# Half of batch one's MLP moved from between the attention units to the seven-product stage behind attention, in a cross-attention block on one Trainium2 core

## The chip, the core and the metric

The kernel runs on one core of one Trainium2 chip. The metric is device time in microseconds (us) of one execution. Five engines work from instruction queues of their own, each in program order: TensorE (PE, matmuls), VectorE (DVE), ScalarE (ACT), GpSimd (POOL) and SyncE (SP, which here only issues DMAs). ACT and POOL issue a few DMAs too. An instruction waits for its inputs and for its output buffer, and everything behind it on its engine waits with it.

## The reference

For each of 4 batches, with 512 queries, 512 keys, width 512, 16 heads of 32 and an inner width of 2048, all in float32:

```python
x = layer_norm(hidden_states, ln1_w, ln1_b)
q, k, v = x @ q_w + q_b, enc @ k_w + k_b, enc @ v_w + v_b      # split into 16 heads
attn = softmax(where(mask, q @ k.T / sqrt(32), min))
hidden = (attn @ v) @ cproj_w + cproj_b + hidden_states
y = layer_norm(hidden, ln2_w, ln2_b)
return hidden + gelu(y @ fc_w + fc_b) @ proj_w + proj_b
```

## The kernel before

**Units, quarters, pairs.** Attention is cut into 16 units w: batch w // 4, and four of the 16 heads. A unit has four quarters of 128 queries; u = 4w + quarter counts them from 0 to 63. In a quarter (`scores`, L233) PE makes the scores of the four heads (`sc`, L240, one PSUM tile of four banks, single-buffered); DVE adds the mask and finds the row extreme (L245); ACT takes the exponential (L249); DVE turns the result in 32x32 blocks into the tile `tb` (`turn`, L253, L277). Two quarters make a **pair** p = 2w + half, with 256 queries.

**The exchange.** The blocks of `tb` lie on the wrong partitions, so the turned pair is copied within on-chip memory by 16 DMAs of 136 KB (`copies`, L305 to L320, all issued by SP), into a tile that `attend` (L342) then multiplies with v (`av`, L362). Pairs 2, 4, 6 are copied into `gt`, pairs 29 and 31 into `xe`; **every other one goes into the tile `pT`, of which there is one**. So `exchange` (L294) holds the next pair's copies back until `attend` of the pair before is through: its last step, the DVE multiply `oT` (L367), reads the last rows of `pT`, and SP's first copy waits for it. `attend` of pair p stands ahead of the scores of quarter 2p + 4 (LAG, L60, L853); for pairs 7 and up that is one `attend` per half unit.

**Work between the units.** Everything else on PE is cut into pieces of four 128x512 matmuls into one PSUM tile, here called **chains**: k, q and v of coming units (L196, L206, L218), the output projection `accc` (L399), and the MLP of batches 0 and 1, `accf` (`fc`, L457) and `accp` (`proj`, L467), 64 chains. The profile counts each f32 matmul as two, so a chain has 8. The lists `first[w]` and `later[w]` (L773 to L843) say which chains a unit gets (`some(n)` takes the next n of the MLP), and the loop at L845 hands them out over the quarters by cost: `CHAIN` is 3.4, a turn of layer norm 0.5. Of the 64 MLP chains 57 stand in units 5 to 15, 7 behind the last unit. MLP weights come in tiles of 256 KB, eight at a time; a chain that has read the last of one lets SP load the next (`load_mlp`, L442).

**Behind attention** (`last_mlps`, L515) batches 2 and 3 are done by seven products of blocks in place of eight: `fc_pair` (L549) makes two of the 16 inner blocks by 14 matmuls of 128x256 (`q`, L561), `project` (L592) the projection by seven products (q1p to q7p, L601). The sums of blocks that this needs are made by DVE: `sum_wa` (fc weights), `y_sums`, `g_sums`, `p_sums` (projection weights). `project` ends with the work for the next batch: after q5p, `middle` queues `y_sums` and `sum_wa(0)` on DVE, PE does q4p, and the third product of the next `fc_pair` reads `s4`, the last result of `sum_wa(0)`.

**Before the last stage** PE does, in this order: 2 MLP chains, `attend` of pair 30, 4 chains, `attend` of pair 31, 1 chain, the four `accc` of batch 3.

Of the kernel before, what the change touches and what calls it, by code (L numbers as in the profile page):

```python
# [55 lines left out]
AHEAD = 3  # L58
NORMAL = 2
LAG = 4  # L60
# [14 lines left out]
def xattn_block(ctx: ExitStack, tc: tile.TileContext, x, encT, mask, q_w, k_w, v_w, c_w, fc_w, p_w, vecs, rows, out):  # L75
# [10 lines left out]
    att = ctx.enter_context(ExitStack())  # L86
    one, two, kqp, five, six, fws = pools(att, one=1, two=2, kqp=4, five=5, six=6, fws=MW)
    ps_sc = att.enter_context(tc.tile_pool(name="ps_sc", bufs=1, space=PSUM))
# [14 lines left out]
    gT = [gt[:, i * FQ * L : (i + 1) * FQ * L].rearrange("p (k l) -> p k l", k=FQ) for i in range(2)]  # L103

    S = {}
    Q = [nc.sync]

# [73 lines left out]
    def load_w(w, queue=None, names=("wk", "wq", "wv")):  # L181

        if w >= NW:
            return
        g = w % NG
        for n, src in (("wk", k_w), ("wq", q_w), ("wv", v_w)):
            if n in names:
                S[n, w] = two.tile([P, ND, P], F32, tag=n, name=f"{n}_{w}")
                (queue or Q[0]).dma_start(out=S[n, w], in_=src[:, g, :, :])

    def prep_k(w):
        b, g = divmod(w, NG)
        kT = kqp.tile([P, L], F32, tag="kT", name=f"kT_{w}")
        acc = acc_tile(f"acck_{w}")
        for d in range(ND):
            nc.tensor.matmul(acc, S["wk", w][:, d, :], eT[:, d, :], start=(d == 0), stop=(d == ND - 1))  # L196
        load_w(w + 2, names=("wk",))
        nc.scalar.activation(kT, acc, AF.Identity, bias=vec[:, KB + g : KB + g + 1], scale=1.0)
        S["kT", w] = kT

    def prep_q(w):
        b, g = divmod(w, NG)
        qT = kqp.tile([P, L], F32, tag="qT", name=f"qT_{w}")
        acc = acc_tile(f"accq_{w}")
        for d in range(ND):
            nc.tensor.matmul(acc, S["wq", w][:, d, :], xT[:, d, :], start=(d == 0), stop=(d == ND - 1))  # L206
        load_w(w + 2, names=("wq",))

        nc.scalar.activation(qT, acc, AF.Identity, bias=qb[:, g : g + 1], scale=-scale)  # L209
        S["qT", w] = qT  # L210
# [22 lines left out]
    def scores(w, qt):  # L233
# [8 lines left out]
        for h in range(HG):  # L242
            s = six.tile([P, L], F32, tag="s", name=f"s_{w}_{qt}_{h}")
            mn = small.tile([P, 1], F32, tag="mn", name=f"mn_{w}_{qt}_{h}")
            nc.vector.tensor_tensor_reduce(  # L245
                out=s, in0=sc[:, h, :], in1=S["mb", w // NG], scale=1.0, scalar=FMAX,
                op0=ALU.add, op1=ALU.min, accum_out=mn,
            )
            nc.scalar.activation(s, s, AF.Exp, bias=mn, scale=-1.0, accum_out=sums[:, qt, h : h + 1])  # L249
            ps.append(s)  # L250
# [125 lines left out]
    def stays(b, t):  # L376

        return b == 0 or b < B - 1 and t < 2

    def load_h(b, *ts_):  # L380
# [3 lines left out]
        for t in ts_:  # L384
            pool, tag = (hids, "hid") if stays(b, t) else (tiles, "xn")
            S["h", b, t] = pool.tile([P, D], F32, tag=tag, name=f"h_{b}_{t}")
            Q[0].dma_start(out=S["h", b, t], in_=x[b, ts(t, P), :])
            if stays(b, t):
                S["hid", b, t] = S["h", b, t]
# [5 lines left out]
    def cproj(b, t):  # L395
# [5 lines left out]
        if not stays(b, t):  # L401
            (nc.sync if b == B - 1 else nc.gpsimd).dma_start(out=S["xa", b][ts(t, P), :], in_=h)

    def load_hid(b, ts_):
# [28 lines left out]
    weights, products = [], []  # L433
    for b in range(NORMAL):
        for name, q in (("fc", 0), ("fc", 1), ("p", 0), ("fc", 2), ("p", 1), ("fc", 3), ("p", 2), ("p", 3)):
            for k in range(FQ):
                last = len(products) + (k if name == "fc" else NT - 1)
                weights.append((name, b, q * FQ + k, last))
            products += [(name, b, q, k) for k in range(FQ)]
    count = [0, 0]  # L440

    def load_mlp():  # L442

        while count[0] < len(weights) and (count[0] < MW or weights[count[0] - MW][3] < count[1]):
            name, b, f, _ = weights[count[0]]
            w = fws.tile([P, D], F32, tag="mw", name=f"{name}w_{b}_{f}")
            if name == "fc":
# [63 lines left out]
    def sum_wa(c):  # L511
        a = wa[c % 2]
        a_sums(a[:, 0, :2], a[:, 0, 2:], a[:, 1, :2], a[:, 1, 2:], *(ws[c % 2][:, i] for i in range(4)))

    def last_mlps():  # L515
        last, ring = pools(ctx, last=1, ring=2)
# [3 lines left out]
        gs = last.tile([P, 3, NP, HL], F32, tag="gs", name="gs")  # L520
        pb = last.tile([P, NP, 2, D], F32, tag="pb", name="pb")
        pt = last.tile([P, 3, NP, HL], F32, tag="pt", name="pt")
        hl = last.tile([P, NT, D], F32, tag="hl", name="hl")
        p1p, u2p, u3p = (last.tile([P, 2, HL], F32, tag=n, name=n) for n in ("p1p", "u2p", "u3p"))

# [11 lines left out]

        def p_sums(c):

            c = slice(c, c + 2)  # L540
            b11, b12, b21, b22 = (pb[:, c, k, j * HL : (j + 1) * HL] for k in range(2) for j in range(2))
            b_sums(b11, b12, b21, b22, pt[:, 0, c], pt[:, 1, c], b12, pt[:, 2, c])

        def g_sums(c):
# [3 lines left out]

        def fc_pair(b, c, sums):  # L549
            a11, a12, a21, a22 = (wa[c % 2][:, i, 2 * k : 2 * k + 2] for i in range(2) for k in range(2))  # L550
# [23 lines left out]

            if c == 0:
                product(q43[:, 1], s4, y22)
# [7 lines left out]
            gelu(1, 1, uc[:, 0])  # L584
            if c:
                product(q43[:, 1], s4, y22)
# [4 lines left out]

        def project(b, sums, turns, middle):  # L592
            g11, g12, g21, g22 = (ga[:, :, k, j * HL : (j + 1) * HL] for j in range(2) for k in range(2))
# [4 lines left out]
            def product(o, a, w, ts_=range(2)):  # L598
                for t in ts_:
                    for c in range(NP):  # L600
                        nc.tensor.matmul(o[:, t], a[:, c, ts(t, P)], w[:, c], start=(c == 0), stop=(c == NP - 1))  # L601

# [46 lines left out]

        y_sums(NORMAL)  # L650
        for t in range(NT):
            S["hid", B - 1, t] = hl[:, t]
        for b in range(NORMAL, B):
            for c in range(NP):
                if b == NORMAL:
                    for i in range(2):
                        nc.sync.dma_start(out=pb[:, c, i, :], in_=p_w[ts(2 * c + i, P), :])
                fc_pair(b, c, lambda: sum_wa(c + 1) if c + 1 < NP else None)
                if c + 2 < NP:
                    load_wa(c + 2)  # L660
                elif b + 1 < B:
                    load_wa(c + 2 - NP)
                if c % 2 == 0 and c:
                    g_sums(c - 2)

                if b + 1 < B:
                    for t in {0: (0,), 1: (1, 2), 3: (3,)}.get(c, ()):
# [6 lines left out]

            def sums(b=b):
                if b == NORMAL:
                    for c in range(0, NP, 2):
                        p_sums(c)
                if b + 1 < B:
                    load_hid(b + 1, range(NT))  # L680

            def turns(b=b):
                if b + 1 < B:
                    run(turns2(b + 1))

            def middle(b=b):
# [3 lines left out]

            project(b, sums, turns, middle)

# [89 lines left out]
    mlp = []  # L782
    for p in range(NORMAL):
        mlp += FC(p, 0) + FC(p, 1) + PJ(p, 0) + FC(p, 2) + PJ(p, 1) + FC(p, 3) + PJ(p, 2) + PJ(p, 3)

    def some(n):
# [31 lines left out]
    k, q, v = A(8)  # L818
    first[5] = norm(0, 0, 1, 2, 3) + [q, k] + t2[:3] + [v] + t2[3:] + pb_(0) + some(5)
    k, q, v = A(9)  # L820
    x1, x2, x3, x4 = inputs(3)
    first[6] = [k, q] + some(5) + [v] + x1
    k, q, v = A(10)
    first[7] = [k, q] + x2[:1] + some(3) + x2[1:2] + some(3) + [v]

# [3 lines left out]
    k, q, v = A(12)  # L829
    first[9] = [q] + some(2) + [k] + some(3) + [v]  # L830
    k, q, v = A(13)
    first[10] = [k, q] + some(5) + [v]
    k, q, v = A(14)
    t2 = turns2(1)
    first[11] = stat(1, 0, 1) + [k, q] + stat(1, 2, 3) + rs(1) + some(2) + norm(1, 0, 1) + some(1)
    first[11] += norm(1, 2, 3) + some(2) + t2 + pb_(1) + [v]

    k, q, v = A(15)
    first[12] = h_(2, 2, 3, 0, 1) + [k] + some(3)
    later[12] = cb(2) + C(2)  # L840
    first[13] = hid_(1, 2, 3) + [q] + some(3) + [v] + some(3)
    first[14] = some(5) + stat(2, 0, 1) + some(2) + stat(2, 2, 3) + rs(2) + some(1)
    first[15] = norm(2, 0, 1) + some(4) + norm(2, 2, 3) + some(4) + turns2(2) + pb_(2)  # L843

# [31 lines left out]

    load_h(B - 1, *range(NT))
    run(some(2))
    turn_sums(NW - 1, 0)
    attend(NW - 1, 0)  # L880
    run(some(2))
    load_wa(0)
    run(some(2))
    turn_sums(NW - 1, 1)
    attend(NW - 1, 1)
    run(some(2))
    load_wa(1)
    sum_wa(0)
    c_bias(B - 1)
    run(C(B - 1))  # L890
    load_hid(NORMAL, (2, 3))
    att.close()
# [45 lines left out]
```

## Time and profile before

| | |
|---|---|
| median of 3 runs | 826.09 us (825.77 to 826.44) |
| the profiled execution | 823.17 us, its span 821.4 us |
| PE | 805.0 us busy, 98% of the span |
| DVE, ACT, POOL | 562.7, 347.7, 90.4 us busy |
| DMA | 134.91 MB, mean 164 GB/s |
| units 1 to 15, start of the first scores to the end of the last | 52.26 to 572.0 us |
| stage of seven products | 622.7 to 818.1 us |

The profile is of one execution. Its page gives busy time by engine and by 40 equal slices, and the chain that ended last, followed back from the last instruction. The trace behind it answers for a stretch of time with the instructions of one engine, and ahead of each the idle time and what ended it. A PE matmul's listed length is longer than its spacing, since matmuls are pipelined; lengths here are differences of starts.

### The profile page before, as it was taken

What the parts mean: (1) busy time and instruction counts of PE and PEld (TensorE: products, weight loads), DVE (VectorE), ACT (ScalarE), POOL (GpSimd) and SP (SyncE); (2) the same over time, 40 slices, a digit from 0 to 9 for tenths busy, and PEclk for the clock granted to TensorE, in tenths of its full rate; (3) what the DMA queues carried; (4) which work ended last, traced back from release to release, by engine and by line L of the source; (5) the groups of instructions that cost most, each with busy time, mean ns of one, the idle gap of its engine ahead of it and who ended that gap; (6) DMA issues with size and microseconds to landing.
All of it is one profiled execution on the core that took longest, in us unless ns stands there. A gap on an engine that the chain in (4) does not pass through costs nothing.

```text
span 821.4 us, 11900 instructions
## 1 busy us (share of the span) xinstructions
PE 805.0 (98%) x4020; PEld 467.0 (57%) x4020; DVE 562.7 (69%) x1264; ACT 347.7 (42%) x741; POOL 90.4 (11%) x98
## 2 busy tenths in 40 slices
PE   9998999999999999999999999999999999999998
PEld 6553545454454554454544444434447888888887
DVE  3598989886576778667886667787426986268511
ACT  2455555346554744365435367556201331023200
POOL 1110003112000111000111210010201012200011
PEclk9998999999999999999999999999999999999999
DMA  9639998856668768677676676777734550023001
GB/s 327 231 88 237 239 247 233 218 147 161 173 164 222 183 166 237 162 209 194 159 212 179 157 197 159 199 181 174 211 116 162 193 171 14 26 77 89 2 13 39
DMA packets 59740, 134.91 MB, mean 164 GB/s; under 512 B 12144, under 2 KB 14320, under 8 KB 59552
## 3 DMA queue, kind: packets, MB, share of 16 engines
q1 hardware_dynamic: 58416, 130.73, 58.8%
q0 software_dynamic: 736, 2.29, 0.8%
q10 hardware_dynamic: 528, 1.14, 0.5%
q8 instruction: 32, 0.52, 0.3%
q14 instruction: 28, 0.23, 0.1%
HBM read 58.74 MB, written 6.29 MB: 79 GB/s over the span
## 4 chain that ended last, share of the span: by engine, by line
PE 85%; DMA 5%; DVE 5%; SPq 3%; issue 1%; ACT 1%; DVEq 0%; ACTq 0%
PE accp L467 14%; PE accf L457 14%; PE q L561 12%; PE sc L240 7%; PE accc L399 7%; PE av L362 6%; PE accv L218 4%; PE acck L196 4%; PE accq L206 4%; SPq L319 3%; PE q4p L601 2%; PE q3p L601 2%; PE q7p L601 2%; PE q2p L601 2%; PE q5p L601 2%; PE q6p L601 2%
## 5 line engine op out<-in xcount | busy, mean ns | idle before, releaser
L249 ACT ACTIVATE s<-s,mn 128x512 f32<-128x512 f32 x256 | 181.6, 710 | 138.0 <-DVE mn L245 137.8
L245 DVE CUSTOM_DVE_ANT_0 s<-sc,mb 128x512 f32<-128x512 f32 x256 | 161.3, 686 | 55.4 <-PE sc L240 55.2
L277 DVE STREAM_TRANSPOSE tb<-s 128x512 f32<-128x512 f32 x248 | 161.6, 690 | 9.5 <-ACT s L249 8.5
L457 PE MATMUL accf<-yT,fcw 128*128 128x512 f32 x256 | 115.5, 599 | 0.5 <-ACT v L223 0.3
L467 PE MATMUL accp<-pw,gt 128*128 128x512 f32 x256 | 115.0, 598 | 0.0
L457 PEld LDWEIGHTS accf<-yT,fcw 128*128 128x128 f32 x256 | 47.2, 190 | 65.5 <-issue 55.5
L467 PEld LDWEIGHTS accp<-pw,gt 128*128 128x128 f32 x256 | 47.2, 190 | 63.8 <-issue 61.1
L240 PE MATMUL sc<-kT,qT 32*128 32x512 f32 x512 | 73.8, 646 | 1.1 <-ACT qT L209 0.8
L218 PEld LDWEIGHTS accv<-wv,xe 128*128 128x128 f32 x512 | 58.8, 192 | 9.9 <-issue 6.2
L218 PE MATMUL accv<-wv,xe 128*128 128x128 f32 x512 | 60.7, 277 | 1.7 <-ACT xe L142 0.9
L362 PE MATMUL av<-pT,v 128*32 128x256 f32 x864 | 53.9, 391 | 6.7 <-DMA pT<-tb 6.7
L561 PE MATMUL q<-ys,gt 128*128 128x256 f32 x256 | 60.1, 379 | 0.0
L196 PE MATMUL acck<-xe,wk 128*128 128x512 f32 x128 | 59.6, 609 | 0.0
L206 PE MATMUL accq<-xe,wq 128*128 128x512 f32 x128 | 58.5, 599 | 0.0
L399 PE MATMUL accc<-wc,oT 128*128 128x512 f32 x128 | 56.9, 597 | 0.0
L561 PEld LDWEIGHTS q<-ys,gt 128*128 128x128 f32 x256 | 48.6, 190 | 6.6
L249 ACT ACT_TABLE_LOAD x22 | 28.2, 1283 | 52.7 <-DVE mn L245 52.7
L230 POOL TENSOR_TENSOR v<-v,row 128x512 f32<-128x512 f32 x16 | 20.3, 1269 | 261.5 <-ACT v L223 261.4
L249 ACT ACTIVATION_READ_ACCUMULATOR s<-s,mn 128x1 f32 x256 | 47.7, 187 | 0.0
L362 PEld LDWEIGHTS av<-pT,v 128*32 128x32 f32 x864 | 26.1, 112 | 36.7 <-issue 18.9
L561 PE MATMUL q<-yT,gt 128*128 128x256 f32 x192 | 46.3, 379 | 0.0
L367 DVE TENSOR_TENSOR oT<-av,pT 128x256 f32<-128x256 f32 x26 | 11.0, 422 | 46.7 <-PE av L362 43.9
(117 smaller groups left out, 855.2 us busy)
## 6 DMA issues: line engine op xcount, KB each, us to landing
pT<-tb SPq DMA_DIRECT2D x416, 136.0 KB, 2.4
fcw<-fc_w_dram SPq DMA_DIRECT2D x32, 256.0 KB, 3.4
pw<-p_w_dram SPq DMA_DIRECT2D x32, 256.0 KB, 3.5
gt<-fc_w_dram SPq DMA_DIRECT2D x32, 256.0 KB, 3.0
gt<-tb SPq DMA_DIRECT2D x48, 136.0 KB, 2.8
wk<-k_w_dram SPq DMA_DIRECT2D x16, 256.0 KB, 3.5
xe<-encT_dram SPq DMA_DIRECT2D x16, 256.0 KB, 6.0
wv<-v_w_dram SPq DMA_DIRECT2D x16, 256.0 KB, 3.1
```

Source lines behind the costliest of these rows:

```text
L196: nc.tensor.matmul(acc, S["wk", w][:, d, :], eT[:, d, :], start=(d == 0), stop=(d == ND - 1))
L218: nc.tensor.matmul(acc[:, ts(t, P)], eT[:, d, ts(t, P)], S["wv", w][:, d, :], start=(d == 0), stop=(d == ND - 1),)
L240: nc.tensor.matmul(sc[:, h, :], qT[r, ts(qt, P)], kT[r, :], start=True, stop=True)
L245: nc.vector.tensor_tensor_reduce(out=s, in0=sc[:, h, :], in1=S["mb", w // NG], scale=1.0, scalar=FMAX, op0=ALU.add, op1=ALU.min, accum_out=mn,
L249: nc.scalar.activation(s, s, AF.Exp, bias=mn, scale=-1.0, accum_out=sums[:, qt, h : h + 1])
L277: nc.vector.transpose(tv[:, q, h], S["ps", w, qt][h])
L362: nc.tensor.matmul(av[ts(h, HD), : 2 * P].rearrange(shape, **kw), v[:, t, ts(h, HD)], p[t][h], start=(t == 0), stop=(t == NT - 1),)
L399: nc.tensor.matmul(acc, S["oT", b][:, g, ts(t, P)], wc[:, g, :], start=(g == 0), stop=(g == NG - 1))
L457: nc.tensor.matmul(acc, S["fcw", b, f][:, d, :], S["yT", b][:, d, :], start=(d == 0), stop=(d == ND - 1))
L467: nc.tensor.matmul(acc, gT[q % 2][:, k, ts(t, P)], S["pw", b, q * FQ + k], start=(k == 0), stop=(k == FQ - 1))
L561: nc.tensor.matmul(o, a[:, k], y[:, k], start=(k == 0), stop=(k == 1))
L601: nc.tensor.matmul(o[:, t], a[:, c, ts(t, P)], w[:, c], start=(c == 0), stop=(c == NP - 1))
```

## The change

Batch 1 (`SPLIT`) is done by chains only up to the second quarter of its inner width (`FIRST` = 2 of 4): 16 of its 32 chains leave the list, and last_mlps begins with batch 1 and the inner pairs 4 to 7. The units get 41 MLP chains in place of 57: one fewer in units 5, 6, 7, 9, 10, 11 and 12, three fewer in each of 13, 14 and 15.

For this the weights of both stages lie in two tiles that are held throughout: `pbt` (16 slots: k and q of four units in slots 0 to 7, the eight MLP weight tiles in slots 8 to 15; later the projection weights of the seven products) and `ptt` (12 slots: six score tiles and two units' k, q, v weights; later the sums of projection weights). Each of these rings has as many places as its pool had. The projection weights of batch 1's second half are loaded into slots 8 to 15 as the last chains free them, and `p_sums` runs on DVE behind the last unit. The layer norm turns of batch 2 move from unit 15 into batch 1's `project`. Batch 3's hidden rows go to DRAM and come back (`load_xn`), because they are first made in slots of `pbt`. Batch 2's rows are read back whole into `hl`.

```diff
-NORMAL = 2
+SPLIT = 1
+FIRST = 2
...
-    one, two, kqp, five, six, fws = pools(att, one=1, two=2, kqp=4, five=5, six=6, fws=MW)
+    one, two, five = pools(att, one=1, two=2, five=5)
...
+    pbt = const.tile([P, NF * D], F32, tag="pbt", name="pbt")
+    ptt = const.tile([P, 3 * (NF // 2) * (D // 2)], F32, tag="ptt", name="ptt")
...
+    def k_q(w, i):
+        n = w % 4 * 2 + i
+        return pbt[:, n * D : (n + 1) * D]
+
+    def mlp_w(n):
+        n = n % MW + MW
+        return pbt[:, n * D : (n + 1) * D]
...
+    def load_xn(b):
+
+        for t in range(NT):
+            S["h", b, t] = tiles.tile([P, D], F32, tag="xn", name=f"hn_{b}_{t}")
+            Q[0].dma_start(out=S["h", b, t], in_=S["xa", b][ts(t, P), :])
...
+    weights += [("p", SPLIT, FIRST * FQ + k, None) for k in range(MW)]
...
-        for b in range(NORMAL, B):
-            for c in range(NP):
-                if b == NORMAL:
+        half = FIRST * FQ // 2
+        for b, pairs, new in (
+            (SPLIT, range(half, NP), ()), (SPLIT + 1, range(NP), range(half)), (SPLIT + 2, range(NP), ())
+        ):
+            for c in pairs:
+                if c in new:
...
             def turns(b=b):
                 if b + 1 < B:
                     run(turns2(b + 1))
+                if b == SPLIT:
+                    load_xn(B - 1)
...
-    for p in range(NORMAL):
+    for p in range(SPLIT):
         mlp += FC(p, 0) + FC(p, 1) + PJ(p, 0) + FC(p, 2) + PJ(p, 1) + FC(p, 3) + PJ(p, 2) + PJ(p, 3)
+    mlp += FC(SPLIT, 0) + FC(SPLIT, 1) + PJ(SPLIT, 0) + PJ(SPLIT, 1)
...
-    first[12] = h_(2, 2, 3, 0, 1) + [k] + some(3)
+    first[12] = h_(2, 2, 3, 0, 1) + [k] + some(2)
     later[12] = cb(2) + C(2)
-    first[13] = hid_(1, 2, 3) + [q] + some(3) + [v] + some(3)
-    first[14] = some(5) + stat(2, 0, 1) + some(2) + stat(2, 2, 3) + rs(2) + some(1)
-    first[15] = norm(2, 0, 1) + some(4) + norm(2, 2, 3) + some(4) + turns2(2) + pb_(2)
+    first[13] = [q] + some(1) + stat(2, 0, 1) + [v] + some(2) + stat(2, 2, 3) + rs(2)
+    first[14] = some(2) + norm(2, 0, 1) + some(1) + norm(2, 2, 3) + some(2) + h_(B - 1, *range(NT))
+    first[15] = hid_(1, 2, 3) + some(5) + cb(B - 1)
...
-    load_h(B - 1, *range(NT))
+    first_c = FIRST * FQ // 2
     run(some(2))
-    turn_sums(NW - 1, 0)
     attend(NW - 1, 0)
     run(some(2))
-    load_wa(0)
+    load_wa(first_c)
     run(some(2))
-    turn_sums(NW - 1, 1)
+    p_sums(first_c)
     attend(NW - 1, 1)
-    run(some(2))
-    load_wa(1)
-    sum_wa(0)
-    c_bias(B - 1)
-    run(C(B - 1))
-    load_hid(NORMAL, (2, 3))
+    run(mlp)
+    load_wa(first_c + 1)
+    sum_wa(first_c)
+    c = C(B - 1)
+    run(c[:2])
+    p_sums(first_c + 2)
+    run(c[2:])
     att.close()
     last_mlps()
```

## The prediction

> **What bounds the kernel now.** I read the page's busy time and slices first, then the list of PE's waits, then stretches of the trace by engine, and last the order in which the changed program puts its instructions on each engine.
>
> ```profile
> PE 805.0 (98%) x4020; PEld 467.0 (57%) x4020; DVE 562.7 (69%) x1264; ACT 347.7 (42%) x741; POOL 90.4 (11%) x98
> PE   9998999999999999999999999999999999999998
> DVE  3598989886576778667886667787426986268511
> ```
>
> PE is full in every slice, so work taken from PE is worth its own length, as long as PE stays full. What PE waits for in all 16 units, and the second of these waits in PE's order of time:
>
> ```profile
> PE av L362 <- DMA pT<-tb: 6.7, 2, 3.4
> ...
> 138.07 3.84 PE L218 MATMUL accv<-wv,xe 128*128 128x128 f32 x32
> 145.31 1.93 PE L362 MATMUL av<-pT,v 128*32 128x256 f32 x32 [3.40 <-DMA pT<-tb]
> ```
>
> The only long waits are for the copies of the exchange, and they fell where units were short (units 1 to 3 took 24 to 26 us; those from 6 on about 36). So the second thing to know is how short a half unit may be. A half of unit 14, PE first, then DVE, then SP:
>
> ```profile
> 506.46 1.93 PE L362 MATMUL av<-pT,v 128*32 128x256 f32 x32
> 508.33 1.14 PE L240 MATMUL sc<-kT,qT 32*128 32x512 f32 x8
> 509.40 7.13 PE L467 MATMUL accp<-pw,gt 128*128 128x512 f32 x16
> 516.46 1.14 PE L240 MATMUL sc<-kT,qT 32*128 32x512 f32 x8
> ...
> 524.60 1.93 PE L362 MATMUL av<-pT,v 128*32 128x256 f32 x32
> ```
> ```profile
> 508.46 0.42 DVE L367 TENSOR_TENSOR oT<-av,pT 128x256 f32<-128x256 f32 x1 [1.20 <-PE av L362]
> ```
> ```profile
> 508.92 10.03 SPq L319 DMA_DIRECT2D pT<-tb  x16
> ```
>
> The half lasts 18.14 us from `av` to `av`. Inside it runs a loop that PE does not see: oT ends 2.42 us after `av` starts, SP's first copy follows 0.04 later, the 16 issues take 10.03, and the last one lands. How long that takes shows where PE waited: issues from 132.72 for 10.29, `av` at 145.31, so 2.30 after the issues' end. The loop is 2.42 + 0.04 + 10.03 + 2.30 = **14.79 us**. It is hidden by 3.3 us now. With one `pT` it is the shortest time from one `attend` to the next.
>
> **What is taken from PE and given to it.** The end of the list of what ended last:
>
> ```profile
> 608.97 13.73 PE accc L399 x32
> 622.71 48.35 PE q L561 x224
> 671.05 6.91 PE q1p L601 x32
> ```
>
> - Removed: 16 chains of 8 matmuls; 32 of them took 13.73, so 3.43 a chain, 54.9 us.
> - Added: four `fc_pair` of 28, at 48.35/224 = 0.216 each, 24.2 us; seven products over four inner pairs in place of eight, half of 6.91 each, 24.2 us. Together 48.4.
> - Difference: **-6.5 us**. Transposes, scores, k, q, v and `accc` keep their number.
>
> **The seam between batch 1 and 2.** q4p covers the sums for the next batch. Before, DVE began the q5p joins at 714.57, `y_sums` and `sum_wa(0)` ended at 720.0, and PE asked for s4 at 721.20 + 4 x 2 x 0.216 = 722.9. With q4p halved PE asks 3.45 earlier, at 719.5: **+0.6 us** (bounds 0, if the joins start sooner, and 1.5, if POOL's joins come late).
>
> **The shorter halves.** From rows above, `av` to next scores is 1.87, a quarter's scores 1.07, the first chain behind them 3.63, a further one 3.43. A half of 4 chains is then 18.13 (seen: 18.14), of **3 chains 14.70, of 2 chains 11.27**. The changed order gives: 3 chains in the second halves of units 6, 9, 10 and the first of 12, 13, 14; 2 chains in the second halves of 13 and 14, all between `attend`s that use `pT`. (Unit 15's halves end at pairs 29 and 30: 29 has its own place and its copies start as soon as its turns are done; the walk below leaves it 2 us to spare.) Each is held against 14.79:
>
> - Second halves of 13 and 14: 14.79 - 11.27 = 3.5 each, 7.0.
> - First halves of 13 and 14: 0.1 each by the loop. But DVE is late too. A quarter costs DVE 4 x (0.615 + 0.69) plus starts, about 5.7, a pair's sums 0.9; unit 13 also gets layer norm statistics (0.67 + 0.18 each, four) and three adds of 0.69, and all of that stands ahead of oT. Walking DVE from the first oT of unit 13, with its waits, oT is 0.2 late after the first half and 0.6 after the second, and the next copies start that much late. Four halves together: 0.1 + 3.6 + 0.7 + 3.5 = **7.9 us**.
> - First half of 12: ahead of oT stand two turns of 0.79, the mask at 1.02 and late exponent work of unit 11's last quarter; by the same walk oT is 2.2 late, and the 3-chain half has nothing to give: **+1.9** (bounds 0 and 2.5).
> - Second halves of 6, 9, 10: 0.1 by the loop; issue times of 16 copies were 10.03 to 11.45, mostly 10.03: **+0.7** (0 to 4).
>
> At the end of unit 14 six weight loads (1.5 MB) stand on SP between two sets of copies. Four loads of x right ahead of copies at 245.29 left these at 10.03; in the early units copies behind loads took 12.27 and 13.28. So 0 to 3.2 for that one place; I take 0, the row that is nearest in kind.
>
> Sum: -6.5 + 0.6 + 7.9 + 1.9 + 0.7 = **+4.6 us**. The profiled execution took 823.17 (821.4 span), 2.9 under the median; a difference is the same on both, so 823.17 becomes 827.8, and the median **826.1 becomes 830.7**.
>
> [...]
>
> **Costed at nothing, and by what cover.**
> - Rings laid in `pbt` and `ptt`: as many places as before, and the waits printed for the changed program name the same engines. If a slot were tied to a neighbour's reader, each unit would show it.
> - `p_sums` behind the last unit: 8 sums of 0.69, 5.5 us on DVE, which there stands idle 2.74 of every 3.43. oT of pair 31 queues behind four of them, and `accc` needs it only at its fourth matmul pair, behind one more chain: 4 us to spare, if the projection weights (loaded as chain 44 of 48 frees them) land within 6 us; 256 KB loads took 3.5.
> - Batch 3's rows over DRAM: loaded in batch 1's `project`, used one `fc_pair` into batch 2, some 20 us later.
> - Batch 3's loads of x and two of batch 1's rows now stand on SP ahead of pair 30's copies (some 4 us of issue); pair 30 is due 6 us after they land by the walk.
> - Batch 2's turns move with their 1.75 us of PE. ACT's table loads (1.28 each) in units 14 and 15 fit beside the waits.
>
> **The rivals.**
> 1. *Faster.* The loop is not that stiff: the copies need DMA time, not SP time, and land sooner when nothing else is moved. Place: the `attend`s of units 13 and 14. For it: pair 31's 16 copies, split over SP and ACT, were issued in 6.73 us, so the DMA engines can do more. Against: they stay on SP alone, at about 0.63 an issue, in all units, busy or not. The stalls of two-chain halves are 2 x (loop - 11.27); with DVE's lateness of some 1 us the change gains over 0.2% if the loop is under about 12.9, and all of it below 11.3: -6.5 + 0.6, **820.2**. Chance 0.20.
> 2. *About even.* DVE is less late than in my walk and the three-chain halves just fit: only 2 x 3.5 is lost. -5.9 + 7.0 = +1.1, **827.2**. For it: 14.70 and 14.79 differ by less than I know them. Chance 0.16.
> 3. *Slower still.* The copies behind the six loads take 13.28 (+3.2), and each of the other tight halves has an issue time of 11.45 (+1.4, four of them, less the 0.7 counted): +4.6 + 3.2 + 4.9, **838.8** at worst, about 836. Chance 0.08.
> 4. That the change doesn't do what it says: the changed order has 41 chains in the units and 7 behind them, so I give it no chance of its own.
>
> The forecast has the remaining 0.56. Measured differences under 0.2% (1.65 us) can't be told from none. Faster: rival 1, 0.20. Same: rival 2, 0.16. Slower: the forecast and rival 3, 0.64. The range goes down into rival 1, to 821.5, and up to 835, between the forecast and the worst case; the forecast's own is 827.8 to 835.
>
> **What the changed profile would show.** PE's waits for `pT` at some 17 us in place of 6.7, the new ones ahead of `av` at the ends of units 13 and 14, 3 to 4 us each, and one near 2 us at unit 12's middle; 16 copies issued in 10 to 11 us throughout; the stage of seven products 48.4 us longer, with under 1 us of idle at the first `fc_pair` of batch 2; units 5 to 15 shorter by some 45 us rather than 55. If `av` shows no wait in units 13 and 14, the loop was wrong; if it shows waits for DVE, my prices of DVE were; if PE waits in the tail, the covers named above were.

## The result, and the profile after

The changed kernel takes **834.58 us** (median of 8 runs, 829.14 to 837.01); the kernel before took 825.51 in the same comparison (8 runs, 824.24 to 826.44). The ratio is **1.0102, 95% interval [1.0074, 1.0131]**: slower by 9.1 us, where the prediction had 4.6. The profiled execution took 836.84 us (span 835.1), 13.7 more than that of the kernel before. Of all runs below, one execution of g2_turns_alone (1382 us, mean granted clock 0.56) was in a slow state and stays out of the figures.

The page of the changed kernel, first the busy time and then slices:

```profile
PE 803.5 (96%) x4116; PEld 488.7 (59%) x4116; DVE 576.6 (69%) x1312; ACT 341.2 (41%) x746; POOL 96.5 (12%) x108
...
PE   9897998999999999999899988999999999999998
...
PEclk9999999999999999999999989999999999999999
```

PE is busy 1.5 us less than before and the program is longer: the time is in waits. A second thing is in the last line: one slice has a clock under 0.9, and it is where PE waits. The list of PE's waits (in all, times, longest):

```profile
PE av L390 <- DMA pT<-tb: 11.8, 4, 4.3
PE av L390 <- DMA ptt<-v_w_dram: 3.4, 1, 3.4
PE accv L246 <- ACT yT L170: 3.2, 1, 3.2
```

The second line is the stall of unit 4 that stood before too (145.31 there). Units 13 and 14 in PE's timeline (start, duration, wait in brackets), where the kernel before had no wait:

```profile
468.20 1.93 PE L390 MATMUL av<-pT,v 128*32 128x256 f32 x32 [0.65 <-PE accv L246]
...
483.81 3.64 PE L390 MATMUL av<-pT,v 128*32 128x256 f32 x32 [4.27 <-DMA pT<-tb]
487.38 2.02 PE L268 MATMUL sc<-pbt 32*128 32x512 f32 x8
...
501.09 1.93 PE L390 MATMUL av<-pT,v 128*32 128x256 f32 x32
...
515.87 3.08 PE L390 MATMUL av<-pT,v 128*32 128x256 f32 x32 [3.44 <-DMA pT<-tb]
518.88 1.63 PE L268 MATMUL sc<-pbt 32*128 32x512 f32 x8
...
532.21 1.93 PE L390 MATMUL av<-xe,v 128*32 128x256 f32 x32
```

Both two-chain halves end in the wait that was forecast, 4.27 and 3.44 us. But read the second column too: behind each wait an attend takes 3.64 or 3.08 us in place of 1.93 and the scores 2.02 or 1.63 in place of 1.14. The same stretches by window (PE, PEld, DVE, ACT and POOL busy, then the granted clock) say why:

```profile
470.00:500.00 30.00, 25.73 (x106) 10.11 (x103) 24.64 (x62) 13.13 (x34) 2.93 (x5) 0.89 0.70 178
500.00:530.00 30.00, 26.56 (x135) 10.70 (x134) 21.95 (x56) 22.18 (x39) 0.00 (x0) 0.94 0.90 230
```

The clock was 0.89 and 0.94. So each of these stalls cost its own length and some us of slower matmuls behind it: 1.71 + 0.88 = 2.6 behind the first, 1.15 + 0.49 = 1.6 behind the second.

The last third of unit 11 was not in the prediction at all. POOL, DVE, ACT and PE there, in four answers:

```profile
406.30 2.91 POOL L402 TENSOR_TENSOR h<-h,row 128x512 f32<-128x512 f32 x2 [6.63 <-DVE xn L156]
```
```profile
405.72 0.96 DVE L156 TENSOR_SCALAR xn<-h,mv,rs 128x512 f32<-128x512 f32 x2
...
407.19 2.30 DVE L156 TENSOR_SCALAR h<-h,mv,rs 128x512 f32<-128x512 f32 x2
```
```profile
412.86 0.71 ACT L277 ACTIVATE ptt<-ptt,mn 128x512 f32<-128x512 f32 x1
413.48 0.19 ACT L277 ACTIVATION_READ_ACCUMULATOR ptt<-ptt,mn 128x1 f32 x1
413.57 1.42 ACT L170 ACTIVATE yT<-tp,vec 128x512 f32<-128x512 f32 x2
```
```profile
414.38 5.32 PE L246 MATMUL accv<-ptt,xe 128*128 128x128 f32 x32 [3.19 <-ACT yT L170]
```

Four turns of layer norm fill the ring of four PSUM tiles; the `v` behind them needs the first tile back; ACT empties it, but only behind four exps, and it waits 6.21 us for DVE ahead of the first of them (410.73). PE waits 3.19 us, and 5.32 instead of 3.84 follow at a lower clock (0.72 from 414 to 420 us). The chain that the change took from between the norms and the turns used to cover this; before, the wait here was 0.87:

```profile
430.02 3.84 PE L218 MATMUL accv<-wv,xe 128*128 128x128 f32 x32 [0.87 <-ACT yT L142]
```

The stage at the end is as forecast (from the chain that ended last, within 560 to 720 us):

```profile
585.43 24.17 PE q L601 x112
609.61 3.45 PE q1p L641 x16
...
637.94 46.89 PE q L601 x216
```

Four pairs in 24.17 us and products over four inner pairs at 3.45 each (6.91 over eight) are the new work. The seam is a wait of 0.5 us (`q` on `gt`).

**Where the 13.7 us are.** By the starts of three attends (8, 31, the end) the profiled executions split so: up to attend 8, 168.91 against 165.19, +3.7; from there to attend 31, 397.22 against 438.22, -41.0; from there to the end 268.97 against 217.99, +51.0. The middle part by window, the kernel before first:

```profile
165.19:603.41 438.22, 435.49 (x2106) 200.33 (x2105) 308.06 (x714) 229.32 (x461) 47.88 (x47) 1.00 0.71 183
```
```profile
168.91:566.13 397.22, 383.18 (x1961) 178.20 (x1960) 293.11 (x704) 210.10 (x442) 46.38 (x47) 0.98 0.75 194
```

PE's work there shrank by 16 chains and the turns, 54.9 + 1.75 = 56.7 us. Its busy time shrank by 52.3 only: I put the other 4.3 us down to the clock (1.00 and 0.98 above). Its idle time rose from 2.73 to 14.04: 11.3 us are waits. Together 15.6 us of cover lost, against 10.5 in the prediction. The first part, +3.7, is taken up at e4_layout.

### The profile page after: what moved, and what is told of

Its sections match the earlier page's. It is cut to its first block, busy times and chain, and to the rows that moved or that the text cites. A ratio compares the mean times of both kernels' runs of the same rounds, so it can differ in the third digit from the quotient of the medians.

```text
span 835.1 us, 11960 instructions
## 1 busy us (share of the span) xinstructions
PE 803.5 (96%) x4116; PEld 488.7 (59%) x4116; DVE 576.6 (69%) x1312; ACT 341.2 (41%) x746; POOL 96.5 (12%) x108
## 3 DMA queue, kind: packets, MB, share of 16 engines
q10 hardware_dynamic: 528, 1.14, 0.6%
## 4 chain that ended last, share of the span: by engine, by line
PE 79%; SPq 7%; DMA 7%; DVE 4%; issue 1%; ACT 1%; DVEq 0%; ACTq 0%
PE q L601 14%; PE accf L497 9%; PE accp L507 7%; PE av L390 7%; SPq L347 7%; PE accc L431 7%; PE sc L268 6%; PE acck L224 5%; PE accq L234 5%; PE accv L246 5%; PE q5p L641 2%; PE q3p L641 2%; PE q7p L641 2%; PE q6p L641 2%; PE q2p L641 2%; PE q1p L641 2%
## 5 line engine op out<-in xcount | busy, mean ns | idle before, releaser
L277 ACT ACTIVATE ptt<-ptt,mn 128x512 f32<-128x512 f32 x256 | 181.6, 710 | 173.4 <-DVE mn L273 173.3
L273 DVE CUSTOM_DVE_ANT_0 ptt<-sc,mb 128x512 f32<-128x512 f32 x256 | 161.1, 685 | 41.0 <-PE sc L268 40.8
L305 DVE STREAM_TRANSPOSE tb<-ptt 128x512 f32<-128x512 f32 x248 | 157.2, 683 | 7.3 <-ACT ptt L277 4.5
L497 PE MATMUL accf<-yT,pbt 128*128 128x512 f32 x192 | 87.0, 601 | 0.0
L507 PE MATMUL accp<-pbt,gt 128*128 128x512 f32 x192 | 86.3, 600 | 0.0
L268 PE MATMUL sc<-pbt 32*128 32x512 f32 x512 | 75.6, 661 | 1.1 <-ACT pbt L237 0.8
L246 PEld LDWEIGHTS accv<-ptt,xe 128*128 128x128 f32 x512 | 60.3, 196 | 12.7 <-issue 5.2
L246 PE MATMUL accv<-ptt,xe 128*128 128x128 f32 x512 | 62.2, 281 | 4.4 <-ACT yT L170 3.2
L224 PE MATMUL acck<-xe,ptt 128*128 128x512 f32 x128 | 58.9, 602 | 0.0
L234 PE MATMUL accq<-xe,ptt 128*128 128x512 f32 x128 | 58.6, 600 | 0.0
```

Source lines behind the costliest of these rows:

```text
L246: nc.tensor.matmul(acc[:, ts(t, P)], eT[:, d, ts(t, P)], S["wv", w][:, d, :], start=(d == 0), stop=(d == ND - 1),)
L268: nc.tensor.matmul(sc[:, h, :], qT[r, ts(qt, P)], kT[r, :], start=True, stop=True)
L273: nc.vector.tensor_tensor_reduce(out=s, in0=sc[:, h, :], in1=S["mb", w // NG], scale=1.0, scalar=FMAX, op0=ALU.add, op1=ALU.min, accum_out=mn,
L305: nc.vector.transpose(tv[:, q, h], S["ps", w, qt][h])
L497: nc.tensor.matmul(acc, S["fcw", b, f][:, d, :], S["yT", b][:, d, :], start=(d == 0), stop=(d == ND - 1))
L507: nc.tensor.matmul(acc, gT[q % 2][:, k, ts(t, P)], S["pw", b, q * FQ + k], start=(k == 0), stop=(k == FQ - 1))
```

## The experiments

My theory (A): the size was missed by the clock behind the stalls and by unit 11, and the loop of `pT` stands as described. Rivals: the time is set elsewhere, by the transfers themselves (in f3_act) or by DVE and ACT, late wherever the chains stand (B), or the new memory layout costs something (C). Each experiment was measured beside the kernel before.

### e1_even: no half with two chains

```diff
-    first[7] = [k, q] + x2[:1] + some(2) + x2[1:2] + some(3) + [v]
+    first[7] = [k, q] + x2[:1] + some(2) + x2[1:2] + some(2) + [v]
-    first[8] = ... + x3[:2] + some(1) + x3[2:] + [v] + ...
+    first[8] = ... + x3[:2] + x3[2:] + [v] + ...
-    first[13] = ... + [v] + some(2) + stat(2, 2, 3) + rs(2)
-    first[14] = ... + norm(2, 2, 3) + some(2) + h_(B - 1, *range(NT))
+    first[13] = ... + [v] + some(3) + stat(2, 2, 3) + rs(2)
+    first[14] = ... + norm(2, 2, 3) + some(3) + h_(B - 1, *range(NT))
```

> The changed kernel with its 41 chains spread otherwise: one fewer in units 7 and 8, one more in units 13 and 14, so that no half unit has fewer than three. Theory A (the loop of pT stops PE in the two-chain halves, and each such stop also costs clock behind it: in the changed kernel's profile 4.3 + 2.6 us and 3.4 + 1.6 us): both waits ahead of av in units 13 and 14 are gone, the three-chain halves wait under 1 us each, 834.6 falls to 823 to 825. Theory B (DVE and ACT are late in the units, wherever the chains stand): at most 3 us less, 831 to 835. Theory C (the two tiles that hold both stages slow the units down): no change, 834.

Measured: **826.48 us** (823.69 to 828.51, 12 runs), ratio 1.0001 [0.9983, 1.0018]. PE in unit 13 and the first half of 14:

```profile
458.69 1.93 PE L390 MATMUL av<-pT,v 128*32 128x256 f32 x32
...
473.39 1.93 PE L390 MATMUL av<-pT,v 128*32 128x256 f32 x32
...
490.20 2.67 PE L390 MATMUL av<-pT,v 128*32 128x256 f32 x32 [2.04 <-DMA pT<-tb]
```

The same work with its chains spread gives 8.1 us back: nearly the whole loss was where chains were missing, not what was moved. Neither B (at most 3 us back) nor C (none) allows that. A three-chain half now lasts its bare 14.70 us, twice, but the half from 473.39 waits 2.04 us: SP's 16 issues took 11.34 us there instead of 10.05, and began 0.6 us late, because `oT` stood behind layer norm statistics on DVE. The edit also made a stall of its own. The chain that it took from unit 8 stood among four turns of layer norm, and now `v` waits there as in unit 11, 2.55 us, with slower matmuls behind (5.46 us for 3.84):

```profile
282.28 5.46 PE L246 MATMUL accv<-ptt,xe 128*128 128x128 f32 x32 [2.55 <-ACT xe L170]
```

That half of unit 8 fell only from 21.48 to 20.98 us, though a chain of 3.43 us left it. These two places are enough for the 1.5 us above the upper end of A's range. Unit 11 still waits, 2.60 us.

### e2_xe27: the tile of one more pair out of the loop

```diff
-IN_XE = (29, 31)
+IN_XE = (27, 29, 31)
```

> The changed kernel with pair 27 copied into xe, which is free by then, in place of pT; nothing else. Theory A: the copies of pair 28 no longer wait for the attend of pair 27, so the wait at the end of unit 14 (3.4 us, and 1.6 of clock behind it) goes and the one at the end of unit 13 stays (pair 26 still follows pair 25 in pT): 834.6 falls by 4 to 5.5, to about 829.5. Theory B and C: under 1 us.

Measured: **831.31 us** (830.19 to 834.57, 6 runs), ratio 1.0067 [1.0042, 1.0092], 3.3 less than the changed kernel, a little short of A's 4 to 5.5.

```profile
482.44 3.64 PE L390 MATMUL av<-pT,v 128*32 128x256 f32 x32 [4.33 <-DMA pT<-tb]
...
499.50 1.93 PE L390 MATMUL av<-xe,v 128*32 128x256 f32 x32
...
511.36 1.93 PE L390 MATMUL av<-pT,v 128*32 128x256 f32 x32 [0.52 <-DMA pT<-tb]
```

With pair 27 in a tile of its own, pair 28 may follow 11.86 us behind it, not 14.78, and its wait falls from 3.44 to 0.52. It is the single `pT` that sets the distance of two attends. Pair 26 stays in the loop and waits as before.

### e3_idle: the same stalls, filled with matmuls that nobody reads

```diff
+            if pair in (26, 28):
+                idle = acc_tile(f"idle_{pair}")
+                for _ in range(4):
+                    nc.tensor.matmul(idle, ident, row[:, 0, :], start=True, stop=True)
```

> The changed kernel with four extra matmuls (identity by a constant row, 3.4 us, results unused) on PE just ahead of the attends of pairs 26 and 28, where PE stands still anyway. Theory A with the clock: the copies land no sooner, but PE does not stand still, so the granted clock stays at 1 and the av and scores behind it run at 1.86 and 1.07: 2.6 + 1.6 us less, 834.6 to about 830.5. A loop without a clock cost: no change, or up to 0.5 more. If PE did not in fact wait there: 6.8 more, 841.

Measured: **831.86 us** (828.13 to 833.41, 6 runs), ratio 1.0067 [1.0041, 1.0093], 2.7 less.

```profile
483.01 1.93 PE L390 MATMUL av<-pT,v 128*32 128x256 f32 x32 [0.86 <-DMA pT<-tb]
...
513.39 1.93 PE L390 MATMUL av<-pT,v 128*32 128x256 f32 x32
```

By the medians, added work made the kernel faster. The halves still end when the copies land (15.63 and 14.77 us from attend to attend, against 15.61 and 14.78), so the copies came no sooner; the attends behind them take 1.93 us again, and the clock is 1.00 in both windows. The halves that follow took 15.61 and 14.70 us, where they had taken 17.28 and 16.34: the clock's term by itself, 3.3 us in these two traces. The first of them gave back 1.7 of its 2.6 us only, since this three-chain half now ran into the loop and ended 0.9 us above its bare 14.70. The intervals of e2_xe27, e3_idle and, below, g2_turns_alone overlap that of the changed kernel, [1.0074, 1.0131], so for the size of each of these gains the traces say more than the medians.

### e4_layout: the old schedule in the new memory layout

The kernel before, with the weights and `q`, `k`, `exp` tiles laid in `pbt` and `ptt` as the change does, and nothing moved.

> The kernel before with the memory of both stages in pbt and ptt (the same slots for scores, k, q, weights and sums), and its own schedule: 57 chains in the units, batches 2 and 3 by seven products. Theory C: units 0 to 4 end 3.7 us later as in the changed kernel's profile, 829 or more. Theory A: the layout costs nothing, 825 to 826, within 0.2% of the kernel before; the 3.7 us were that execution's own.

Measured: **824.94 us** (822.96 to 826.46, 12 runs), ratio 0.9991 [0.9976, 1.0006]. The layout costs nothing that can be measured; C falls. Its attend 8 came at 165.31 us, as early as in the kernel before. In the nine profiled executions that run the changed kernel's program up to there, attend 8 came anywhere from 165.70 to 170.51 us. So I take most of the +3.7 us for chance (the last section shows how such differences arise). All nine are later than the 165.19 and 165.31 of the old schedule, which are both from executions faster than their kernel's median; a small steady part is not excluded.

### f1_bias: POOL's addition behind the `v` of unit 11

```diff
-    first[11] += norm(1, 2, 3) + some(1) + t2 + pb_(1) + [v]
+    first[11] += norm(1, 2, 3) + some(1) + t2 + [v] + pb_(1)
```

> The changed kernel with one edit: in unit 11 the two additions of the second bias on POOL (2.91 us for both) come behind the v of unit 15 instead of ahead of it. Theory A (they run beside DVE's last two norms and stretch these from 0.96 to 2.30 us, so the maxima, the exps and the yT copy behind them in ACT's order are late and TensorE waits 3.19 us for the PSUM tile at L246, with 1.5 us more for the lower clock behind it): the norms take 1.0 us again, the wait falls to 1 to 2 us, and the time falls by 2.5 to 4.5 us, to 830 to 832. Rival (ACT's own order is the cause, with two table loads and eight exps ahead of the yT copy; POOL's addition only lies beside it): the norms are short, the wait stays at 2.5 to 3.2 us and the time within 1.5 us of the changed kernel's 834.6.

Measured: **833.54 us** (831.76 to 835.2, 6 runs), ratio 1.0086 [1.0062, 1.011]. DVE and PE, in two answers:

```profile
405.40 1.00 DVE L156 TENSOR_SCALAR h<-h,mv,rs 128x512 f32<-128x512 f32 x2
```
```profile
411.58 3.84 PE L246 MATMUL accv<-ptt,xe 128*128 128x128 f32 x32 [2.55 <-ACT yT L170]
```

My theory of this place fell. The norms are short again (1.00 for 2.30), so the additions did stretch them, but the wait only went from 3.19 to 2.55, and the 1.0 us gained can't be told from none: the two kernels' intervals overlap widely. In the trace this half fell from 21.84 to 19.35 us, but 1.5 of that is the clock behind the wait (`v` takes 3.84 us for 5.32; from 390 to 440 us the clock is 1.00 for 0.97). The rival fits: DVE, and the exps with it, are not late here (DVE waits 0.20 us for the scores), and the copy still stands behind four exps in ACT's order. No run changed that order itself; the next one changes what stands ahead of `v` on PE.

### g2_turns_alone: `v` between the turns

```diff
-    first[11] += norm(1, 2, 3) + some(1) + t2 + pb_(1) + [v]
+    first[11] += norm(1, 2, 3) + some(1) + t2[:2] + [v] + t2[2:] + pb_(1)
```

> The changed kernel with the order of unit 11 alone changed: v between the second and the third turn, the bias on POOL at the end. Theory A (this wait is a term of its own, 3.19 us and 1.5 us of lower clock behind it, that the chain taken from between the norms and the turns had covered): 829.5 to 831 us. Rival (only the POOL's addition counted, as f1_bias gave 1 us): 833 to 834.6.

Measured: median **831.10 us** (825.46 to 835.45, 11 runs), ratio 1.0058 [1.0035, 1.0082], 3.5 less than the changed kernel and 2.4 less than f1_bias, whose move is in it. In its trace the wait at L246 of unit 11 is gone, and this half (attend 21 to 22) lasts 16.54 us, where it took 21.84. With two turns ahead of it `v` takes the third tile of the ring and does not ask for the first one back. Unit 11 was a term of its own. A little of it moves on: the half behind it, the first of unit 12, takes 15.52 us, where it took 14.89.

### f3_act: half of the copies issued by ACT

```diff
-                q = nc.scalar if w == NW - 1 and half and i % 2 else nc.sync
+                q = nc.scalar if pair in (26, 28, 31) and i % 2 else nc.sync
```

> The changed kernel with one edit: of the 16 copies of pT for pairs 26 and 28, the eight with odd i are issued by ACT instead of SP; chains and order stay as they are. Theory A (the 10.03 us in which SP issues 16 copies one behind another set the loop of 14.79 us that the halves with two chains, 11.27 us, can't fill): the copies of both pairs are issued within 5.5 to 7 us, the waits of 4.27 and 3.44 us at pairs 26 and 28 fall to 0 to 1.5 us, and the lower clock behind them with them; less 1 to 3 us for exps that stand behind ACT's eight issues, 826 to 830 us. Rival 1 (the time is the transfers' own: DMA engines 0.9 busy in this stretch): the copies land as late as before, the waits stay above 3 us, 833 to 836. Rival 2 (ACT is late by its eight issues, about 5 us each time, and the turns with it): the waits move to the next pair, 832 to 838.

Measured: **844.63 us** (840.88 to 846.18, 6 runs), ratio 1.0213 [1.0184, 1.0242]. ACT's queue, then PE:

```profile
472.08 7.78 ACTq L347 DMA_DIRECT2D pT<-tb  x8
...
508.46 8.47 ACTq L347 DMA_DIRECT2D pT<-tb  x8
```
```profile
483.85 3.57 PE L390 MATMUL av<-pT,v 128*32 128x256 f32 x32 [2.88 <-DMA pT<-tb]
...
495.22 1.14 PE L268 MATMUL sc<-pbt 32*128 32x512 f32 x8 [3.10 <-DVE mn L273]
```

Slower by 10 us, beyond what even Rival 2 had. The queues of 8 shown take 7.8 to 8.8 us: half the issues for each queue, but near 1 us apiece instead of 0.63. So half the issues on SP did not mean half the time. That the transfers have a part in the loop would fit; it is not shown. The kernel before could have shown this. ACT issues half of pair 31's copies there, and the prediction's 6.73 us for that pair is SP's half alone; all 16 took from 578.74 to 589.56, 10.8 us:

```profile
578.74 6.73 SPq L319 DMA_DIRECT2D xe<-tb  x8
```
```profile
580.99 8.57 ACTq L319 DMA_DIRECT2D xe<-tb  x8
```

Pair 26's wait fell from 4.27 to 2.88 only, and pair 28's rose from 3.44 to 3.86, now put down to ACT. In the 7.78 and 8.47 us in which ACT issues it does no exps, and scores of unit 14 wait 3.10 us for DVE (495.22), a stall that was not there. ACT's own lateness and the slower issues are mixed in this run; it does not say how much of the loop the transfers are.

### f2_all and g1_turns: the repairs together

f2_all is e1_even with the edits of e2_xe27 and f1_bias; g1_turns is f2_all with `v` between the turns in unit 11 (as in g2_turns_alone) and in unit 8:

```diff
-    first[8] = ... + [k, q] + x3[:2] + x3[2:] + [v] + h_(1, 2, 3) + x4
+    first[8] = ... + [k, q] + x3[:2] + [v] + x3[2:] + h_(1, 2, 3) + x4
```

> Three edits together: the chains spread so that no half has fewer than three (as in the run e1_even, 826.5), pT of pair 27 in xe (as in e2_xe27), and the bias of unit 11 behind v (as in f1_bias). Theory A (the stalls are separate and each is paid where it stands): against e1_even's profile the wait of 2.04 us at pair 27 and 1.6 us of lower clock behind it go, and of 3.4 us in unit 11 some 2 to 3; 819.5 to 821.5 us, 4 to 6 us below the kernel before. Rival (the loop of pT carries one half's lateness into the next, so a wait that is taken away returns at the pair behind it): 824.5 to 827, no better than e1_even.

> The version f2_all with two orders changed: in units 8 and 11 the v projection stands between the second and the third of four turns instead of behind the fourth, so that it needs a third PSUM tile where it needed the fifth of a ring of four. Theory A (TensorE waits 2.55 and 2.72 us at L246 because the tile it needs is emptied by an ACT copy that stands behind four exps in ACT's order): both waits fall below 0.5 us, 4 to 5 us less than f2_all, 818.5 to 820.5 us. Rival (the same copies then hold up the next user of the ring, the attend or the next quarter's chain): the wait stands elsewhere and the time is within 1.5 us of f2_all's 823.7.

Measured: f2_all **823.72 us** (819.16 to 830.52, 12 runs), ratio 0.9978 [0.9955, 1.0001]; g1_turns **817.75 us** (816.49 to 818.29, 6 runs), ratio **0.9892 [0.9873, 0.991]**. f2_all fell between the two expectations: the wait at pair 27 is gone (attends at 475.49, 490.19, 504.90), but unit 11 still waits 2.72 and unit 8 (since e1_even's edit) 2.55. In g1_turns both waits for the ring are gone, and its list of PE's waits has no new one above 1.2 us in their place:

```profile
PE av L390 <- DMA ptt<-v_w_dram: 3.9, 1, 3.9
PE av L390 <- DMA pT<-tb: 3.4, 1, 3.4
PE warm L795 <- POOL nhalf L786: 1.3, 1, 1.3
PE av L390 <- DMA pbt<-fc_w_dram: 1.2, 1, 1.2
```

The first two stand in units 4 and 1, as in the kernel before. So the change, with its cover kept and these repairs, beats the kernel before by 1.1%, 8.2 us by the medians and 5.5 by the two profiled spans; the prediction's work and seam make -5.9. That the seven products alone save this is not shown: the kernel before also waits 0.87 us for the ring in each of units 8 and 11, and it was not run with the new orders.

### g3_before_idle and g4_best_idle: unread matmuls in the early units

> The kernel before with four matmuls of 128x512 that nobody reads ahead of the attends of pairs 2, 3 and 7, where its TensorE waits 3.3 us; schedule and other work stay. Theory A (behind a wait of 3 us or more the clock is often lower for some us, in the kernel before as well: 3.64 us for an attend at 66.8 us instead of 1.93): the waits fall to 1 to 1.7 us, clock 1.00 from 40 to 160 us, and the time falls by 1.5 to 3 us, to 823 to 824.5. Rival (the lower clock hides behind the next wait, as the pairs 2 and 3 suggest, and costs nothing): 825.3 to 826.3.

> g1_turns with the same unread matmuls ahead of the attends of pairs 2, 3 and 7. Theory A: 1.5 to 3 us below g1_turns, 816 to 818.5 us, and the clock 1.00 in every stretch. Rival: as g1_turns.

Measured: 828.75 us (826.53 to 830.17, 12 runs), ratio 1.0029 [1.0014, 1.0045], and 822.58 (820.72 to 823.67, 8 runs), 0.9951 [0.9933, 0.9968]. Both slower, by 2.8 and 4.8 us, but they do not test what I meant: I had counted the pairs wrongly. The stall at 66.8 us is pair 1's, so it stayed unfilled, and pair 3 has no stall to fill. In g3_before_idle pairs 2 to 3 take 15.23 us (82.14 to 97.37), where the kernel before took 11.80. That is the length of the four matmuls, 3.43. Pair 7's wait they did fill: 10.14 us from pair 6 to 7, as before (10.17), and `av` took 1.93 there before too. So the unread matmuls helped inside a wait (e3_idle, 2.7 us less), and where there was none they cost their length, 3.43 us. What the lower clock of the early units costs stays open.

## Why the prediction was right, and where its size was off

- **Mechanism and side: right.** The main loss is the two-chain halves against the loop of `pT` (e1_even, e2_xe27). The forecast, 830.7, was 3.9 us short; 834.58 lies just inside the upper end of the range, 835.
- **Work taken and given, -6.5, and the turns: right.** The stage grew by 51.0, where 48.4 + 1.75 + 0.6 = 50.7 were given.
- **Seam, +0.6: right**, 0.5 seen (and 720.0 - 719.5 is 0.5).
- **Four halves of 13 and 14, 7.9: right as waits**, 4.27 + 3.44 + 0.65 = 8.4, **mis-sized as time.** "14.79 - 11.27 = 3.5 each" priced a stall at its length; the clock behind it added 2.6 + 1.6 = 4.2 in this execution, 2.7 by e3_idle's median. I could have read it: in the kernel before, the attend behind the first wait took 3.64 us. I showed the other wait, behind which there was nothing. That the waits alone came so near is partly luck. The late `oT` of my walk (0.2 and 0.6 us) did not come: SP's first copy stood 2.46 us at most behind the start of `av` where `av` was not slowed. In its place pair 25's issues took 10.88 us, and `av` of pair 26 began 2.9 us behind the end of its issues, where the loop had 10.03 and 2.30.

```profile
66.78 3.64 PE L362 MATMUL av<-pT,v 128*32 128x256 f32 x32 [3.34 <-DMA pT<-tb]
```

- **First half of 12, +1.9: wrong.** The half lasted 14.89 us, 0.2 over 14.70. DVE was not late: it stood idle 4.06 us ahead of that `oT`, because PE's wait at the end of unit 11 had let it catch up. Without that wait the half took 15.52 (g2_turns_alone) and 15.31 us (g1_turns), so some 0.6 to 0.8 of lateness was there, not 2.2. The walk of DVE also put a turn of `tb` at its listed 0.69, where four take 2.4 from start to next start, and the mask at 1.02, which took 0.42 here.
- **Second halves of 6, 9, 10, +0.7:** 14.84, 15.61 and 14.84, so 1.2.
- **Second half of 11: not in the sum.** I listed halves by their number of chains against one loop; here the chain removed was the cover of another wait, that for a PSUM tile behind ACT. 3.19 - 0.87 = 2.3 us, and 1.5 of clock; g2_turns_alone gave back 3.5, with the move of f1_bias.
- **Layout at nothing: right** (e4_layout).
- **Rival 1 of the prediction** did not come: the two waits stood. What spoke for it, 6.73 us for pair 31's copies, was a misreading: 6.73 us is SP's half, and the 16 took 10.8 (f3_act).

These losses add up to 17.8 us. Against them, the first half of unit 5 became 1.8 us shorter beyond its chain of 3.43 (22.16 us before, 16.90 after; why is not shown), and 0.4 of the second halves of 6, 9 and 10 had been there before (18.27 for 18.13). That leaves the 15.6 us of lost cover, for 10.5 in the prediction, and turns +4.6 into +9.7; the medians say +9.1. So the total came nearer than its terms: unit 12's 1.9 us were forecast and did not come, unit 11's 3.8 and the clock's 4.2 came and were not forecast.

## What to carry to other kernels

Work that is moved away was also cover: before moving it, list for each stretch every loop and every ring that ran behind it (here one tile's copies, and PSUM tiles emptied by ACT), and hold each against what remains. Price a wait of PE of some 3 us with the slower matmuls that may follow it (1.5 to 2.6 us behind each of the three here), and spread the removals so that no stretch falls below the loop; the same change, with the orders of units 8 and 11 mended and pair 27 out of the loop, then was 1.1% faster instead of 1.0% slower. In a ring of n tiles, don't let n short users that wait for a slow engine stand ahead of a long one: here, with four tiles, PE waited 3.19 us for it in unit 11 and, in e1_even, 2.55 in unit 8.

## What the runs showed of the hardware that was not expected

**The clock behind a wait is partly chance.** In the 13 profiled executions I took all waits of PE from 1.0 us on, behind the first 30 us, and looked whether the matmuls right behind them were longer than usual:

| wait of PE, us | waits | slower matmuls behind |
|---|---|---|
| 1.0 to 1.9 | 21 | 1 |
| 2.0 to 2.75 | 11 | 5 |
| 2.85 to 3.5 | 29 | 19 |
| 3.6 to 4.4 | 9 | 9 |

The same stall of pair 1, 3.32 to 3.38 us in all executions, was followed by an attend 0.5 to 1.7 us slower in six and by a usual one in seven. The seven were not better off: in the six of them without unread matmuls there, pair 2 then waited 2.98 to 4.20 us and its attend was slow instead, and they took 28.8 to 31.1 us from pair 1 to pair 3, where five of the six took 26.8 to 28.6 (the sixth has unread matmuls). That the wider spread of the changed kernel (829 to 837 us) comes from this is argued, not shown. The length of a wait alone does not decide it: of the 40 waits from 2.0 to 3.5 us, 24 were followed by slower matmuls and 16 were not. Why is open.

**DVE and POOL side by side.** Two norms on DVE took 2.30 us beside two additions on POOL, and 1.00 when these were moved (f1_bias).
